# Attention block on one core: query and key projections of two chunks by seven products instead of eight, other order of units, weights read again from DRAM

## Chip, core and metric

The kernel runs on one core of a Trainium2 chip. The metric is device time in microseconds of one execution. Matrix products run on TensorE (PE), elementwise and search work on VectorE (DVE), activations and copies out of PSUM on ScalarE (ACT), more elementwise work on GpSimd (POOL); SyncE (SP) issues nearly all DMAs, in program order.

## The reference

Inputs are `hidden` (4 batches x 1024 rows x 512), weights in float32, and biases. Per batch, cut to what matters here:

```
x = layernorm(hidden)
q  = rope(rmsnorm(x @ Wq  + bq)  * qn_w)      # 512 -> 16 heads x 128
lk = rope(rmsnorm(x @ Wlk + blk) * kn_w)      # 512 -> 16 heads x 128
lv = x @ Wlv + blv
e  = softmax-weighted sums of 4 rows of x     # 256 entries
ck = rope(rmsnorm(e @ Wk + bk)); cv = e @ Wv + bv
sparse: q @ ck / sqrt(128), causal, best 8 entries, softmax, times cv
local:  q @ lk / sqrt(128) over the last 128 positions, softmax, times lv
out = hidden + ((sparse + local) / 2) @ Wo + bo + fp8-rounded x @ fp8-rounded input2
```

## The kernel before

**Chunks and units.** The rows are cut into 32 chunks of 128 (`t`; eight per batch, `c = t % 8`), the 16 heads into eight pairs (`u`). A unit `n = 8 t + u` is one chunk and two heads; there are 256. All weights stay in SBUF: `wqk_sb[u]` holds 512 rows x (256 of Wq, 256 of Wlk), `wlv_sb[u]`, `wo_sb[u]`. The tokens of a chunk, turned, are in `xnT`; `xone` is their first 128 features with one row replaced by ones, for the bias.

**A unit.** `queries` (L606) multiplies the tokens by `wqk_sb[u]`: four matmuls with 512 columns into the PSUM tile `qp`, of which there are two. A float32 matmul appears in the profile as two instructions. `squares` (L321, ScalarE) sums the squares of four heads, `spread` (L315, L316, POOL) turns them into the factors `r`; `normalize` (L634, VectorE) scales `qp` into `th`, `rotate` (L337 on POOL, L339 to L342 on VectorE) applies the angles, `turn_keys` (L687, L690, VectorE) turns blocks of 32x32 into `thb`; SP writes that to DRAM (L695) and reads it back (L705) as `qT` and `lkT`. `scores` (L754, L761, L764) fill `sc`; `weigh` (L786 to L812, VectorE) masks, finds the best eight and their maximum, and ScalarE takes exponentials (L814, L822); `settle` (L830 to L840, VectorE), `divide` (L847, ScalarE); `turn` (L865, VectorE) turns blocks, through DRAM again (L873, L907) into `probT`. `values_of` (L712) makes `vp`, `keep_values` (L724) copies it; `values` (L924) makes the contexts `cp`, `keep_context` (L939) copies them, `to_output` (L957) multiplies by `wo_sb[u]`. PSUM has eight banks: `qp` two, `pp` (values and all short-lived products) two, `sc` two, `ctx` and `out` one each.

**Order.** The order of the instructions on each engine is written out by hand: the loop over steps `s` at the end. Step `s` works on several units at once: scores, weighing, probabilities of unit `s`; normalizing, rotating, turning of `s + 2`; products and squares of `s + 3`; values of `s + 1`; value product of `s - 1`; output of `s - 2`. Every engine goes through its list in order, so a waiting instruction holds what follows it.

**Work once per chunk.** `chunk_prep` (L355 to L432: statistics, normalizing, the weights of the four-row sums) is dealt out over eight steps by the names in `FIRST_HALF` and `SECOND_HALF`; `chunk_eight` with `quantize` (L287 to L298, then L588 and L592) makes the fp8 product, two small parts in each step; `chunk_entries` adds the entries once in four chunks (L536 to L573). In the first eight steps `fold_first_row` (L272) subtracts the first row of each weight matrix and `round_w2` rounds `input2`.

## Time and profile before

| | us |
|---|---|
| median of 3 runs | 2641.59 (2640.97 to 2642.03) |
| span of the profiled execution | 2641.7 |
| VectorE busy in the third batch (643.0 us) | 548.65 |
| ScalarE busy there | 343.79 |
| POOL busy there | 188.74 |
| first eight units after the start, 30 to 123 us | 93.0 |
| second chunk's eight units, 123 to 206 us | 83.0 |

An engine's busy time says how much of a stretch it worked; the waits say which engine it waited for; the timeline gives every instruction's start and length in us. A line such as L606 names the line of the kernel. The times of the profile are of one execution.

### The profile page before, as it was taken

What the parts mean: (1) busy time and instruction counts of PE and PEld (TensorE: products, weight loads), DVE (VectorE), ACT (ScalarE), POOL (GpSimd) and SP (SyncE); (2) the same over time, 40 slices, a digit from 0 to 9 for tenths busy, and PEclk for the clock granted to TensorE, in tenths of its full rate; (3) what the DMA queues carried; (4) which work ended last, traced back from release to release, by engine and by line L of the source; (5) the groups of instructions that cost most, each with busy time, mean ns of one, the idle gap of its engine ahead of it and who ended that gap; (6) DMA issues with size and microseconds to landing.
All of it is one profiled execution on the core that took longest, in us unless ns stands there. A gap on an engine that the chain in (4) does not pass through costs nothing.

```text
span 2641.7 us, 46868 instructions
## 1 busy us (share of the span) xinstructions
PE 2609.3 (99%) x11879; PEld 1784.3 (68%) x11879; DVE 2213.4 (84%) x8381; ACT 1390.9 (53%) x5560; POOL 786.2 (30%) x1128
## 2 busy tenths in 40 slices
PE   8999999999999999999999999999999999999998
PEld 4666666776666666767766666667666666676776
DVE  6888888889888888888888888888888888877886
ACT  3545545555555555555555555555555555555555
POOL 3522323223332223232233322233323322322222
PEclk9999999999999999999999999999999999999999
DMA  8356556666655555666655555666665555566554
GB/s 255 110 156 162 151 145 175 171 176 158 164 143 154 162 155 156 169 173 170 166 157 144 158 149 158 177 164 164 171 176 147 150 148 153 147 168 171 159 152 110
DMA packets 722252, 422.20 MB, mean 160 GB/s; under 512 B 395823, under 2 KB 671552, under 8 KB 721984
## 3 DMA queue, kind: packets, MB, share of 16 engines
q1 hardware_dynamic: 721952, 419.20, 58.8%
q8 instruction: 97, 1.59, 0.3%
q14 instruction: 171, 1.40, 0.2%
q10 hardware_dynamic: 32, 0.02, 0.0%
HBM read 225.80 MB, written 193.20 MB: 159 GB/s over the span
## 4 chain that ended last, share of the span: by engine, by line
PE 84%; DVE 7%; ACT 3%; DMA 3%; SPq 2%; issue 1%; POOL 0%; ACTq 0%; DVEq 0%
PE qp L606 28%; PE op L957 14%; PE vp L712 14%; PE cp L924 13%; PE sc L764 5%; PE sc L761 4%; PE sc L754 4%; ACT prob L847 1%; ACT prob L814 1%; PE fp L588 1%; DVE sc L786 1%; DVE probB L865 1%; PE ep L536 1%; SPq L695 1%; DVE taken L812 1%
## 5 line engine op out<-in xcount | busy, mean ns | idle before, releaser
L606 PE MATMUL qp<-wqk,xnT 128*128 128x512 f32 x1552 | 709.8, 593 | 3.0 <-DMA wqk<-in_L_attn_Wlk_dram 2.4
L814 ACT ACTIVATE prob<-sc,neg 128x256 f32<-128x256 f32 (+1 forms) x512 | 235.9, 461 | 773.3 <-DVE taken L812 744.0
L606 PEld LDWEIGHTS qp<-wqk,xnT 128*128 128x128 f32 x1552 | 295.0, 190 | 372.5 <-issue 368.8
L847 ACT ACTIVATE prob<-prob,tot 128x256 f32<-128x256 f32 (+7 forms) x1024 | 382.0, 443 | 294.5 <-DVE tot L840 294.5
L712 PEld LDWEIGHTS vp<-wlv,xnT 128*128 128x128 f32 x2048 | 389.0, 190 | 161.3 <-issue 116.2
L957 PE MATMUL op<-wo,cT 128*128 128x512 f32 x1024 | 481.6, 593 | 4.2 <-ACT cT L939 4.2
L712 PE MATMUL vp<-wlv,xnT 128*128 128x256 f32 x2048 | 483.6, 379 | 0.0
L337 POOL TENSOR_TENSOR rb<-th,cs 128x256 f32<-128x256 f32 x256 | 203.8, 796 | 740.0 <-DVE th L634 733.2
L786 DVE CUSTOM_DVE_ANT_0 sc<-sc,mask_b 128x256 f32<-128x256 f32 (+1 forms) x512 | 211.6, 414 | 172.7 <-PE sc L764 162.7
L957 PEld LDWEIGHTS op<-wo,cT 128*128 128x128 f32 x1024 | 193.6, 190 | 229.8 <-issue 186.8
L865 DVE STREAM_TRANSPOSE probB<-prob 128x512 f32<-128x512 f32 (+2 forms) x490 | 305.8, 629 | 11.5
L315 POOL TENSOR_SCALAR r<-ss 128x4 f32<-128x4 f32 x256 | 61.9, 242 | 843.3 <-ACT junk L321 840.6
L924 PE MATMUL cp<-probT,lv 128*128 128x128 f32 x1920 | 299.0, 276 | 6.4 <-DMA probT<-pr 4.9
L321 ACT ACTIVATE junk<-qp 128x128 bf16<-128x128 f32 x1024 | 278.6, 272 | 28.9 <-PE qp L614 4.5
L924 PEld LDWEIGHTS cp<-probT,lv 128*128 128x128 f32 x1920 | 272.8, 191 | 25.4 <-issue 9.3
L634 DVE SCALAR_TENSOR_TENSOR th<-qp,r,norm_w 128x128 f32<-128x128 f32 x1024 | 286.1, 342 | 0.7 <-POOL r L316 0.4
L316 POOL TENSOR_TENSOR r<-r,nhalf 128x4 f32<-128x4 f32 x256 | 265.6, 1037 | 21.4
L830 DVE SCALAR_TENSOR_TENSOR prob<-taken,prob 128x128 f32<-128x128 bf16 (+7 forms) x512 | 186.4, 365 | 98.1 <-ACT prob L822 96.6
L606 PE MATMUL qp<-wqk,xone 128*128 128x512 f32 x496 | 258.3, 602 | 0.9 <-DMA xone<-xb_dram 0.7
L924 PE MATMUL cp<-probT,cv 128*128 128x128 f32 x1536 | 255.1, 275 | 0.0
L764 PE MATMUL sc<-ckT,qT 128*128 128x96 f32 (+7 forms) x1024 | 226.4, 303 | 0.0
L924 PEld LDWEIGHTS cp<-probT,cv 128*128 128x128 f32 x1536 | 212.7, 192 | 0.0
(141 smaller groups left out, 3674.9 us busy)
## 6 DMA issues: line engine op xcount, KB each, us to landing
pr<-probB SPq DMA_DIRECT2D x125, 512.0 KB
probT<-pr SPq DMA_DIRECT2D x500, 128.0 KB
qk<-thb SPq DMA_DIRECT2D x992, 64.0 KB
pr<-probB SPq DMA_DIRECT2D x96, 384.0 KB
probT<-pr SPq DMA_DIRECT2D x384, 96.0 KB
qT<-qk SPq DMA_DIRECT2D x248, 128.0 KB
lkT<-qk SPq DMA_DIRECT2D x248, 128.0 KB
x_norm<-_attn_hidden_states_dram SPq DMA_DIRECT2D x32, 256.0 KB
```

The source lines that it names most:

```text
L316: nc.gpsimd.tensor_tensor(r, r, nhalf[: ss.shape[0], 0:n], ALU.pow)
L321: nc.scalar.activation(junk[: src.shape[0]], src, AF.Square, accum_out=acc)
L606: nc.tensor.matmul(qp, xnT[:, k, :] if k or not t else xone, wqk_sb[u][:, k, :], start=(k == 0), stop=(t > 0 and k == KK - 1),)
L634: nc.vector.scalar_tensor_tensor(th[:, i, :], qp[:, ts(i, D)], r[:, i : i + 1], norm_w[:, i // 2, :], ALU.mult, ALU.mult,)
L712: nc.tensor.matmul(vp[:, 0:256], xnT[:, k, :], wlv_sb[u][:, k, :], start=(k == 0), stop=(k == KK - 1),)
L764: nc.tensor.matmul(sc[:, spa], q, ckT[:, 0:m], start=True, stop=True)
L786: nc.vector.tensor_tensor_reduce(sc[h][:, loc], sc[h][:, loc], mask_b[:, loc], -1.0, TAKEN, ALU.add, ALU.min, neg[h][0],)
L814: nc.scalar.activation(probs[h][:, loc], sc[h][:, loc], AF.Exp, bias=neg[h][0], scale=-1.0, accum_out=tot[:, h, 0:1],)
L847: nc.scalar.mul(probs[h][:, cols], probs[h][:, cols], tot[:, h, part : part + 1])
L865: nc.vector.transpose(pb[:, :, ds(h * g, g), :], prob[:, parts[0] * P : (parts[-1] + 1) * P].rearrange("p (g b i) -> p b g i", b=NB, i=BLK),)
L924: nc.tensor.matmul(blocks(cp[:, h, :]), v, probT[:, :, h * len(parts) + i - parts[0], :], start=(i == parts[0]), stop=(i == parts[-1]),)
L957: nc.tensor.matmul(op, cT[:, h, :], wo_sb[u][:, h, :], start=(u == 0 and h == 0), stop=(u == NU - 1 and h == 1),)
```

## The change

The first 16 units (chunks 0 and 1) are done as before. From unit 16 on, units go in pairs: `place(n)` alternates between chunk `2p` and chunk `2p + 1` with the same heads. For the 120 pairs, the tokens of two chunks (256 rows) times `wqk_sb[u]` are seen as 2x2 blocks, 128 rows x 256 features times 256 features x 256 columns, and made of seven block products by Strassen's algorithm in Winograd's form, each two matmuls of 256 columns. `first_products` makes four of them in an even step `s` (for units `s + 4` and `s + 5`), into the two banks `qk_banks`; `first_sums` copies them to the `th` tiles of both units and adds on POOL. `second_products` makes three in the odd step, into the same banks; `second_sums` adds them on VectorE. `squares` and `normalize` then read `th` in SBUF instead of `qp` in PSUM.

The four sums of token blocks are made by `sum_tokens` once for two chunks on POOL. The four sums of weight blocks are made once by `combine_weights` in steps 4 to 8 on POOL, written to DRAM and read back for each pair by `load_combined` (four transfers of 256 KB); the freed parts of `wqk_sb` (`places`) hold them. `wo_sb` has two tiles instead of eight, and `load_wo` reads 512 KB for each pair.

PSUM: `qk_banks` two, `out_banks` two (two chunks' outputs grow side by side), `sc` two, `vc_bank` holds `vp` and `cp` in its halves, `pp` has one bank, and until step 11 also the second output bank. `th`, `lkT`, `lv` and `x` come from hand-made pools, `th` from one of three tiles that gives out the tile last returned. Preparation of chunks starts at the steps in `prep_at`, later the steps `16 p - 2` and `16 p + 5`. Matmuls of the last, partly filled block of entries use only its filled rows.

```diff
-        return work.tile(list(shape), dtype, tag="scratch", name=name, bufs=2)
+        return work.tile(list(shape), dtype, tag="scratch", name=name, bufs=4)
+
+    def bank(name):
+        return psum.tile([P, 512], F32, tag=name, name=name, bufs=1)
+
+    qk_banks = [bank("qk_0"), bank("qk_1")]
+    out_banks = [bank("out_0"), bank("out_1")]
+    vc_bank, pp_bank = bank("vc"), bank("pp")
+    spare_banks = [pp_bank, out_banks[1]]
 
     def pp(name):
-        return psum.tile([P, 512], F32, tag="pp", name=name, bufs=2)
+        spare_banks.append(spare_banks.pop(0))
+        return spare_banks[-1]
...
+    class Pool:
+
+        def __init__(self, tiles, last=0):
+            self.free, self.taken, self.last = list(tiles), {}, last
+
+        def take(self, key):
+            self.taken[key] = self.free.pop(self.last)
+            return self.taken[key]
+
+        def give(self, key):
+            self.free.append(self.taken.pop(key))
...
-    wqk_sb = [const.tile([P, KK, 512], F32, name=f"wqk_{u}") for u in range(NU)]
+    wqk_sb = [const.tile([P, 2, 2, 2, 256], F32, name=f"wqk_{u}") for u in range(NU)]
...
-    wo_sb = [const.tile([P, 2, HID], F32, name=f"wo_{u}") for u in range(NU)]
+    wo_sb = [const.tile([P, 2, HID], F32, name=f"wo_{i}") for i in range(2)]
+    wo_of = {}
+
+    def row_of_weights(u, k):
+        return wqk_sb[u][:, k // 2, :, k % 2, :]
 
...
-    def load_wo(u, engine):
-        engine.dma_start(wo_sb[u], Wo[ts(u, 256), :].rearrange("(h p) n -> p h n", p=P))
+    def load_wo(n, engine):
+        _, u = place(n)
+        w = wo_sb[n % 2 if n < FIRST else n // 2 % 2]
+        wo_of[n] = w
+        if n >= FIRST:
+            wo_of[n + 1] = w
+        engine.dma_start(w, Wo[ts(u, 256), :].rearrange("(h p) n -> p h n", p=P))
...
+    combined = [
+        dram.tile([4, P, 512], F32, tag=f"combined_{u}", name=f"combined_{u}", bufs=1)
+        for u in range(NU)
+    ]
+
+    def flat(v):
+        return v.rearrange("p k n -> p (k n)")
+
+    def combine_weights(u):
+        (b11, b12), (b21, b22) = (
+            [flat(wqk_sb[u][:, j, i]) for i in range(2)] for j in range(2)
+        )
+        one, two = (v.rearrange("p h d -> p (h d)") for v in th_tiles[1:])
+        sub = nc.gpsimd.tensor_tensor
+        sub(one, b12, b11, ALU.subtract)
+        nc.sync.dma_start(combined[u][0], one)
+        sub(two, b22, one, ALU.subtract)
+        nc.sync.dma_start(combined[u][1], two)
+        sub(one, b21, two, ALU.subtract)
+        nc.sync.dma_start(combined[u][3], one)
+        sub(two, b22, b12, ALU.subtract)
+        nc.sync.dma_start(combined[u][2], two)
+
+    places = [flat(wqk_sb[u][:, 0, 1]) for u in range(NU)]
+    token_sums = [
+        v.rearrange("p (k s) -> p k s", k=2)
+        for at in places[4:6]
+        for v in (at[:, 0:256], at[:, 256:512])
+    ]
+
+    def load_combined(u, which):
+        for i in which:
+            nc.sync.dma_start(places[i], combined[u][i])
+
+    def sum_tokens(p, which):
+        (a11, a12), (a21, a22) = ((b[:, 0:3:2, :], b[:, 3:5, :]) for b in (x_bufs(2 * p), x_bufs(2 * p + 1)))
+        s1, s2, s3, s4 = token_sums
+        op = nc.gpsimd.tensor_tensor
+        if which == 0:
+            op(s3, a11, a21, ALU.subtract)
+            op(s1, a21, a22, ALU.add)
+            op(s2, s1, a11, ALU.subtract)
+        else:
+            op(s4, a12, s2, ALU.subtract)
...
+    th_tiles = [const.tile([P, 4, D], F32, name=f"th_{i}") for i in range(3)]
+    sums = const.tile([P, 256], F32, name="sums")
...
-        return divmod(n, NU)
+        if n < FIRST:
+            return divmod(n, NU)
+        p, r = divmod(n, FIRST)
+        return 2 * p + r % 2, r // 2
...
+        "th": Pool(th_tiles[::-1], -1),
...
     def queries(n):
         t, u = place(n)
         xnT, xone = chunks[t]
-        qp = psum.tile([P, 512], F32, tag="qp", name=f"qp_{n}")
+        qp = qk_banks[n % 2] if n != FIRST - 1 else out_banks[1]
...
+    def product(to, a, b):
+        for k in range(2):
+            nc.tensor.matmul(to, a[k], b[:, k, :], start=k == 0, stop=k == 1)
...
+    def first_products(p, u):
+
+        xa, one = chunks[2 * p]
+        s1, s2, s3, _ = token_sums
+        t1, t2, t3, _ = (v.rearrange("p (k n) -> p k n", k=2) for v in places[:4])
+        lo, hi = qk_banks
+        product(lo[:, 0:256], (one, xa[:, 1, :]), wqk_sb[u][:, 0, 0])
+        product(hi[:, 256:512], both(s1), t1)
+        product(lo[:, 256:512], both(s2), t2)
+        product(hi[:, 0:256], both(s3), t3)
+
+    def second_products(p, u):
+        xa, xb = chunks[2 * p][0], chunks[2 * p + 1][0]
+        lo, hi = qk_banks
+        product(lo[:, 0:256], both(xa[:, 2:4, :]), wqk_sb[u][:, 1, 0])
+        product(hi[:, 0:256], both(xb[:, 2:4, :]), places[3].rearrange("p (k n) -> p k n", k=2))
+        product(hi[:, 256:512], both(token_sums[3]), wqk_sb[u][:, 1, 1])
+
+    def quarters(n):
+        return [
+            units[i]["th"].rearrange("p h d -> p (h d)")[:, ts(j, 256)]
+            for i in (n, n + 1)
+            for j in range(2)
+        ]
+
+    def first_sums(n):
+
+        for i in (n, n + 1):
+            units[i] = {"th": pools["th"].take(i)}
+        c11, c12, c21, c22 = quarters(n)
+        lo, hi = qk_banks
+        nc.scalar.copy(c11, lo[:, 0:256])
+        nc.scalar.copy(c22, lo[:, 256:512])
+        nc.scalar.copy(c21, hi[:, 0:256])
+        nc.scalar.copy(c12, hi[:, 256:512])
+        nc.gpsimd.tensor_tensor(sums, c11, c22, ALU.add)
+        nc.gpsimd.tensor_tensor(c21, c21, sums, ALU.add)
+        nc.gpsimd.tensor_tensor(c22, c21, c12, ALU.add)
+        nc.gpsimd.tensor_tensor(c12, c12, sums, ALU.add)
+
+    def second_sums(n):
+        c11, c12, c21, _ = quarters(n)
+        lo, hi = qk_banks
+        nc.vector.tensor_tensor(c11, c11, lo[:, 0:256], ALU.add)
+        nc.vector.tensor_tensor(c21, c21, hi[:, 0:256], ALU.add)
+        nc.vector.tensor_tensor(c12, c12, hi[:, 256:512], ALU.add)
...
     def squares(n, heads):
         w = units[n]
+        w["ss"] = work.tile([P, 4], F32, tag="ss", name=f"ss_{n}")
+        src = w["qp"] if "qp" in w else w["th"]
         for i in heads:
-            square_sum(w["ss"][:, i : i + 1], w["qp"][:, ts(i, D)], f"{n}_{i}")
+            square_sum(w["ss"][:, i : i + 1], src[:, i, :], f"{n}_{i}")
 
     def spread(n):
         w = units[n]
...
 
     def normalize(n):
         w = units[n]
-        qp, r = w.pop("qp"), w["r"]
-        th = work.tile([P, 4, D], F32, tag="th", name=f"th_{n}", bufs=1)
+        r = w["r"]
+        if "qp" in w:
+            qp, th = w.pop("qp"), pools["th"].take(n)
+        else:
+            qp = th = w["th"]
         for i in range(4):
             nc.vector.scalar_tensor_tensor(
                 th[:, i, :],
-                qp[:, ts(i, D)],
+                qp[:, i, :],
                 r[:, i : i + 1],
...
+        pools["th"].give(n)
...
-        vp = pp(f"vp_{n}")
+        vp = vc_bank[:, 0:256]
...
-        cp = psum.tile([P, 2, P], F32, tag="ctx", name=f"cp_{n}", bufs=1)
+        cp = vc_bank[:, 256:512].rearrange("p (h q) -> p h q", h=2)
...
+                    v, rows = cv[i - 2], min(P, m - P * (i - 2))
                 nc.tensor.matmul(
                     blocks(cp[:, h, :]),
-                    v,
-                    probT[:, :, h * len(parts) + i - parts[0], :],
+                    v[0:rows],
+                    probT[0:rows, :, h * len(parts) + i - parts[0], :],
...
+    prep_at = {1: -1, 2: 6, 3: 8, 4: 13, 5: 16, 6: 19, 7: 22}
+    prep_at.update(
+        {2 * p + 4 + i: FIRST * p - 2 + 7 * i for p in range(2, NT // 2 - 2) for i in range(2)}
+    )
...
+    x_sum_at, eight_at, tokens_at, angles_at = {3: 0, 11: 1}, {5: 0, 13: 1}, {2: 1}, {}
+    for p in range(1, NT // 2):
+        x_sum_at.update({FIRST * p + 3: 2 * p, FIRST * p + 10: 2 * p + 1})
+        eight_at.update({FIRST * p + 3: 2 * p, FIRST * p + 11: 2 * p + 1})
+        tokens_at.update({FIRST * p - 8: 2 * p, FIRST * p - 7: 2 * p + 1})
+        angles_at.update({FIRST * p - 8: 2 * p, FIRST * p - 7: 2 * p + 1})
+    eight_at.pop(FIRST * (NT // 2 - 1) + 11)
 
...
+        pair, odd = divmod(s + 4, 2)
+
+        strassen = pair >= NU and pair < NN // 2
+        pair_of = divmod(pair, NU)
...
+        if s >= FIRST - 5:
+            if r == FIRST - 5 and p + 1 < NT // 2:
+                sum_tokens(p + 1, 0)
+            if r == FIRST - 4 and p + 1 < NT // 2:
+                sum_tokens(p + 1, 1)
...
-        if u == 7 and t in made:
+        if s + 3 < FIRST:
+            for_unit(s + 3, (queries,))
+        if strassen and s != FIRST - 4:
+            (second_products if odd else first_products)(*pair_of)
...
             turn(s)
         if s + 2 >= NU:
             for_unit(s + 2, (turn_keys,))
+        if strassen:
+            (second_sums if odd else first_sums)(2 * pair)
         steps()
-        host = t if u < 4 else t + 1
-        if host in ready and s >= -2:
...
         for_unit(s + 3, (squares, (0, 1, 2, 3)), (spread,))
         for_unit(s - 2, (to_output,))
...
+        if 0 <= s <= FIRST:
+            load_wo(s, nc.sync)
+        elif s > FIRST and odd:
+            load_wo(s + 1, nc.sync)
...
+        for v in {4: (0, 1), 5: (2, 3), 6: (4, 5), 7: (6,), 8: (7,)}.get(s, ()):
+            combine_weights(v)
+        if s == FIRST - 5:
+            load_combined(0, range(4))
+            spare_banks[:] = [pp_bank]
+        if strassen:
+            if odd:
+                load_combined((pair_of[1] + 1) % NU, (3,))
+            else:
+                load_combined((pair_of[1] + 1) % NU, (0, 1, 2))
```

## The prediction

> **What bounds the kernel now.** I read the page's busy lines first, then the table of stretches for the third batch (chunks 0 to 7 of 128 rows, eight units each), then the waits, then the timeline of single units.
>
> ```profile
> span 2641.7 us, 46868 instructions
> PE 2609.3 (99%) x11879; PEld 1784.3 (68%) x11879; DVE 2213.4 (84%) x8381; ACT 1390.9 (53%) x5560; POOL 786.2 (30%) x1128
> q1 hardware_dynamic: 721952, 419.20, 58.8%
> L606 PE MATMUL qp<-wqk,xnT 128*128 128x512 f32 x1552 | 709.8, 593 | 3.0 <-DMA wqk<-in_L_attn_Wlk_dram 2.4
> L712 PE MATMUL vp<-wlv,xnT 128*128 128x256 f32 x2048 | 483.6, 379 | 0.0
> L606 PE MATMUL qp<-wqk,xone 128*128 128x512 f32 x496 | 258.3, 602 | 0.9 <-DMA xone<-xb_dram 0.7
> ```
>
> TensorE never rests. A matmul of these shapes shows as two instructions, and their ends overlap, so the price is busy time over count: 512 columns (709.8 + 258.3) / 2048 = 0.473 us, 256 columns 483.6 / 2048 = 0.236 us. The price goes with the columns.
>
> ```profile
> 1356.30:1426.60 70.30, 69.79 (x300) 45.80 (x299) 59.59 (x261) 36.97 (x172) 22.67 (x35) 1.00 0.55 148
> 1426.60:1504.10 77.50, 77.50 (x353) 52.42 (x353) 63.81 (x260) 41.64 (x172) 22.43 (x33) 1.00 0.55 153
> ...
> 1827.20:1911.50 84.30, 84.30 (x391) 58.76 (x390) 74.30 (x261) 44.95 (x172) 24.36 (x33) 1.00 0.64 168
> 1911.50:1999.30 87.80, 87.66 (x398) 60.68 (x397) 76.67 (x267) 46.71 (x176) 25.80 (x37) 1.00 0.62 165
> ```
>
> Columns: stretch, length, then busy time of PE, weight loads, VectorE (DVE), ScalarE (ACT), GpSimd (POOL), clock, DMA share, GB/s. These are chunks 0, 1, 6 and 7; 2 to 5 take 78.1, 80.4, 81.3 and 83.3. Two units, one of each chunk of a pair, so take 18.48, 19.81, 20.58 and 21.51 us for the pairs (0,1), (2,3), (4,5), (6,7); the mean is 643 / 32 = 20.09.
>
> ```profile
> DVE sc L786 <- PE sc L764: 162.7, 166, 2.1
> DVE prob L830 <- ACT prob L822: 96.6, 248, 1.2
> ```
>
> These are VectorE's main waits: for TensorE's scores only 162.7 us in all, 0.6 a unit, and 0.39 us a unit for the exponentials. VectorE, in order, is nearly a second bound.
>
> ```profile
> 1399.94 0.30 DVE L786 CUSTOM_DVE_ANT_0 sc<-sc,mask_b 128x128 f32<-128x128 f32 x1 [1.99 <-PE sc L764]
> 1401.92 1.12 DVE L634 SCALAR_TENSOR_TENSOR th<-qp,r,norm_w 128x128 f32<-128x128 f32 x4
> 1403.12 0.73 POOL L337 TENSOR_TENSOR rb<-th,cs 128x256 f32<-128x256 f32 x1 [3.49 <-DVE th L634]
> 1405.44 0.25 ACT L321 ACTIVATE junk<-qp 128x128 bf16<-128x128 f32 x1
> 1406.27 0.40 DVE L690 STREAM_TRANSPOSE thb<-th 128x256 f32<-128x256 f32 x1
> 1407.07 0.20 POOL L315 TENSOR_SCALAR r<-ss 128x4 f32<-128x4 f32 x1 [3.22 <-ACT junk L321]
> 1407.35 1.05 POOL L316 TENSOR_TENSOR r<-r,nhalf 128x4 f32<-128x4 f32 x1
> ```
>
> One unit of chunk 0 on the timeline (start, length). VectorE weighs scores (L786 to L634, 1.98 us), normalizes and rotates unit n+2 and turns it (L634 to the end of L690, 4.75 us). ScalarE squares and POOL's root r for unit n+3 end at 1408.40, 2.2 us before the next L634 at 1410.64: no cost now.
>
> **The change, part by part.** *TensorE.* A pair's queries and keys go from 16 instructions of 512 columns to 28 of 256: 16 x 0.473 - 28 x 0.236 = 0.96 us less. 120 of the 128 pairs use it: 115 us off an otherwise full TensorE.
>
> *What takes its place.* Per pair, ScalarE gets four 128x256 copies out of PSUM (0.28 us apart, as keep_keys' two copies start in the timeline), POOL four 128x256 sums (0.73 each, the L337 shown), VectorE three sums with one operand in PSUM (0.40 for the first, as L547 with 397 ns, 0.33 for each next, as L687 to L690). Normalizing from SBUF saves 0.11 us a unit (L558, the same operation from SBUF, 314 ns against 342, four times). By busy time all fits: VectorE 2213 + 120 x (1.06 - 0.22) = 2314 us.
>
> The order decides. Call a step even when it issues first_products. Four facts of the changed order: (1) first_products needs the banks that second_sums of the step before has read, and second_sums stands behind VectorE's turn_keys. (2) The buffer into which the first copy goes is the one that turn_keys of the same step has just read, since the pool of three hands out the last one returned; so ScalarE's four copies, and behind them its squares of unit s+3, values and contexts, wait for the end of turn_keys. (3) POOL's four sums wait for two copies and stand ahead of r of unit s+3. (4) VectorE's normalize of s+3, in the odd step, waits for that r, and all its later work is queued behind it; TensorE and the SP queue's stores wait for that in turn. So a pair is one chain:
>
> a. First VectorE sum to normalize, even step: 0.09 (to ScalarE) + 1.54 (four squares, 1405.44 to 1406.98) + 0.10 (squares from SBUF, 306 ns against 272) + 0.09 + 1.33 (r, 1407.07 to 1408.40) + 0.04 = 3.2 us; or the two other sums 0.66 and the weighing, if longer. The weighing, from the fourth unit of each chunk: 1.98, 2.38, 2.52, 2.65, 2.78, 2.91, 3.04, 3.17. So 3.2, 3.2, 3.44, 3.70 for the four pairs.
> b. Normalize to end of turn_keys, even chunk: 4.75, 5.26, 5.82, 5.91, less 0.11.
> c. End of turn_keys to the odd normalize: 0.09 + 0.65 (two copies) + 0.09 + 4 x 0.73 + 3 x 0.08 (the gap of L315 to L316) + 0.08 + 1.33 + 0.04 = 5.45.
> d. The odd chunk's normalize to turn_keys: 5.18, 5.34, 5.76, 6.07, less 0.11 and 0.39, since the exponentials are now ready in time.
> e. First of second_sums: 0.45 with its hand-over.
>
> Sums: 18.42, 19.09, 20.31, 20.97, mean 19.70.
>
> Work that comes once per chunk is on top. VectorE's chunk work in even steps hides in c (5.45 against 2.4 to 3.2 of weighing); in odd steps it stands between second_sums and the weighing. By the groups that is, per 16 units: 2.74 (chunk started in an even step: normalize and turn 1.24, exponentials 0.85, sum 0.65), 2.83 (the other: statistics 0.85, logits 0.73, weights 1.25), two quantizations 2.62, a last sum 0.68: 8.87, or 1.11 a pair, less 0.14 of slack in pair (0,1): 0.97. The second POOL operation of a quantization (1.27) stands between the sums and r, twice per 16 units: 0.32 a pair, of which I take half, since VectorE has chunk work of its own there. A pair: 19.70 + 0.97 + 0.16 = 20.83 against 20.09, 0.74 more; 120 pairs: 89 us.
>
> *POOL against VectorE.* Beside POOL's work L634, one operand in PSUM, ranges from 335 to 352 ns; L830, both in SBUF, from 178 to 1358. Normalize now has both in SBUF. Six POOL operations of quantizations per 16 units start as r ends. Bounds: 0, as L634 now, to 6 x 1.18 / 8 = 0.89 a pair, 106 us. I take 0, as most of r's ends have nothing behind them; the upper end goes into the range.
>
> [...]
>
> [...]
>
> *Start.* combine_weights: 32 POOL operations of 128x512 (1.27, L294) are 41 us in steps 4 to 8, each a unit of 10.4 (the second chunk's 83.0 / 8) in which POOL has 3.1 already. Steps 4 to 6: 10.2 + 3.1 - 10.4 = 2.9 over, three times, 9 us; if each reused buffer waits for its store (2.5 us, twice a weight), 27 or more. Bounds 0 to 35; I take 10.
>
> *At nothing:* weights from DRAM (1 MB of sums and 0.5 MB of Wo a pair, five SP issues of some 0.45 us in a pair whose SP now issues 10 us of 20), asked for two steps ahead; covered by that distance, priced below. The changed places of preparation, one spare bank, and values sharing a bank with contexts are covered by c; uncovered, a wait of TensorE costs its own length in even steps. Fewer rows in the last value matmuls save nothing: columns set the price.
>
> Total: 2641.7 + 89 + 10 = **2740**, made against the profiled 2641.7, which is 0.1 from the median 2641.59.
>
> **Rivals.** *TensorE stays the bound:* 2641.7 - 115 + 10 = 2537, faster. For it: 99% busy and the busy sums. Against: c. It needs a pair's chain at TensorE's 19.13 even with chunk work, 1.7 us shorter. [...]
> *Chunk work hides in the chain's waits:* 19.70 a pair, 120 x 0.39 = 47 less: 2605. Against: facts 1 and 4 leave none in odd steps.
> *DMA becomes the bound:* 189 MB in 92,000 packets more; by packets the 58.8% becomes 66, by bytes 85. If the probabilities then land 1 us past need in each unit, 240 us: 2880. For: the share. Against: they land about 2 us ahead (stored 2 us before the end of an even step, 6.5 to land, used about 6.6 into the odd one).
> *The products are not fewer:* the changed order shows seven products of two matmuls, so this is out.
>
> **How the numbers follow.** Chain with chunk work 0.66 (2680 to 2830), chunk work hidden 0.12, TensorE 0.10, DMA 0.07, break-even 0.05. The range 2600 to 2830 leaves out TensorE's case and DMA's. A difference under 0.2% (5 us) can't be told from none: faster 0.22, same 0.05, slower 0.73.
>
> **What would show it.** Right: POOL's r and VectorE's normalize alternate between early and late; in odd steps VectorE idles 1 to 2 us before normalize, released by POOL's r; ScalarE's first copy waits for turn_keys; TensorE's first product waits for VectorE; TensorE's share falls to 92 to 94%. Wrong: TensorE still 98% or more busy, or POOL's sums done before turn_keys ends, or probT landings as the main wait.

## The result, and the profile after

The changed kernel takes 3063.97 us (median of 4 runs, 3061.54 to 3068.1) against 2641.28 us before in the same job: a ratio of 1.1603, 95% interval 1.1587 to 1.162. The forecast was 2740 us: right in the direction, wrong by a factor of four in the size (+99 against +423), and outside its range. The profiled execution has a span of 3059.8 us. From its page (engine: busy us, share, instructions; queue: packets, MB, share; the chain by engine):

```profile
span 3059.8 us, 52706 instructions
PE 2744.9 (90%) x13266; PEld 2145.8 (70%) x13301; DVE 2385.6 (78%) x8741; ACT 1566.6 (51%) x6032; POOL 1203.3 (39%) x1686
q1 hardware_dynamic: 828176, 621.15, 70.8%
DVE 33%; PE 22%; ACT 13%; DMA 10%; POOL 10%; issue 6%; SPq 5%; ACTq 0%; POOLq 0%; DVEq 0%
```

No engine is full any more: TensorE went from 99% to 90%, and the chain that ends last runs through all of them. TensorE's busy time has even grown, from 2609.3 to 2744.9 us, though 115 us were to be saved: its mean granted clock is 0.957 of full speed against 0.999, and partly filled matmuls turned out dearer (below). The waits that the forecast had named, from the view of waits (us in total, times, longest):

```profile
POOL sums L782 <- ACT th L779: 427.9, 107, 10.9
...
DVE th L432 <- POOL rb L428: 164.2, 22, 9.7
PE qk L742 <- DVE th L790: 149.5, 79, 5.5
DVE sc L969 <- PE sc L945: 125.8, 73, 14.9
...
ACT th L778 <- DVE thb L867: 120.0, 109, 1.4
DVE th L813 <- POOL r L407: 98.5, 89, 3.7
...
POOL wqk L356 <- DMA tokens<-xb_dram: 67.7, 8, 10.4
...
PE vc L1114 <- DMA probT<-pr: 17.4, 21, 2.0
```

ScalarE's first copy waits for the turned keys in 109 of 120 pairs, TensorE's first product for the second sums, VectorE's normalization for `r`: three links of the forecast chain. New are VectorE's wait for `rb`, 7.5 us a time, and POOL's for `tokens`: the longest of the waits for `rb` come where a sum of tokens stands ahead of it on POOL (e1).

One of the shorter pairs, chunks 4 and 5, fifth place of eight (the two steps in which the fifth pair of heads is weighed), as rows of the timeline of VectorE, ScalarE and POOL (start, us, instruction, idle before it and its releaser):

```profile
2047.60 0.38 DVE L790 TENSOR_TENSOR th<-th,qk 128x256 f32<-128x256 f32 x1
...
2048.56 0.67 DVE L494 SCALAR_TENSOR_TENSOR products<-x,wcmp_sb 128x512 f32<-128x512 f32 x1
...
2049.17 0.43 DVE L969 CUSTOM_DVE_ANT_0 sc<-sc,mask_b 128x256 f32<-128x256 f32 x1
...
2051.94 1.13 DVE L813 SCALAR_TENSOR_TENSOR th<-th,r,norm_w 128x128 f32<-128x128 f32 x4
...
2057.15 0.40 DVE L870 STREAM_TRANSPOSE thb<-th 128x256 f32<-128x256 f32 x1
...
2057.34 0.37 ACT L778 COPY th<-qk 128x256 f32<-128x256 f32 x1 [1.18 <-DVE thb L867]
...
2058.06 0.73 POOL L782 TENSOR_TENSOR sums<-th,th 128x256 f32<-128x256 f32 x1 [4.15 <-DVE row L499]
...
2061.56 1.01 POOL L407 TENSOR_TENSOR r<-r,nhalf 128x4 f32<-128x4 f32 x1
...
2062.61 1.14 DVE L813 SCALAR_TENSOR_TENSOR th<-th,r,norm_w 128x128 f32<-128x128 f32 x4 [0.22 <-POOL r L407]
...
2063.83 0.77 POOL L428 TENSOR_TENSOR rb<-th,cs 128x256 f32<-128x256 f32 x1 [1.25 <-DVE th L813]
...
2064.16 0.66 DVE L1013 SCALAR_TENSOR_TENSOR prob<-taken,prob 128x192 f32<-128x192 bf16 x1
...
2068.25 0.38 DVE L790 TENSOR_TENSOR th<-th,qk 128x256 f32<-128x256 f32 x1
```

Read from one L790 to the next this is the forecast's chain: 0.38 for the first sum, 3.96 to the even normalization (a), 5.61 to the end of the turned keys (b), 5.06 through copies, sums and `r` to the odd normalization (c), 5.72 to the end of the next turned keys (d), less 0.08 by which the next L790 begins before that end: 20.65 us in all. This pair has chunk work too: the logits of a chunk (L494) stand ahead of the weighing, which takes 2.77 us from L969 on, and a is 3.96 where the forecast without chunk work has 3.44. So where did the time come from? Taking the same distance for all pairs by their place among the eight of a chunk pair gives the table that settles most (us, means of 14 or 15 pairs each, without the first pair and the last sixth one, which has no sum of tokens; the last column is the mean of all pairs):

| place | 1 | 2 | 3 | 4 | 5 | 6 | 7 | 8 | mean |
|---|---|---|---|---|---|---|---|---|---|
| changed kernel | 20.94 | 21.58 | 24.19 | 24.29 | 20.36 | 28.67 | 23.65 | 21.98 | 23.19 |
| e1, tokens early | 21.01 | 21.82 | 24.20 | 24.30 | 20.42 | 23.44 | 24.09 | 22.00 | 22.68 |
| e14, fourth buffer | 20.40 | 21.41 | 23.28 | 23.36 | 20.20 | 28.93 | 22.65 | 21.06 | 22.64 |
| e15, no first sums | 20.27 | 21.23 | 22.76 | 21.79 | 20.01 | 30.07 | 22.98 | 20.63 | 22.42 |
| e17, chunk work ahead | 20.93 | 21.95 | 23.70 | 21.62 | 21.30 | 28.76 | 23.31 | 21.73 | 22.88 |

The forecast mean was 20.83, of which 1.13 for work that comes once per chunk. No place is free of chunk work: every one has some on VectorE, and the fifth has at least the logits. The best place, 20.36, is 0.66 above the forecast's 19.70 without chunk work; the excess of the other places over it is 22.8 us in eight pairs, 2.85 a pair. The first sixteen units, from the first weighing to that of unit 16, take 249 us against 176 before.

### The profile page after: what moved, and what is told of

It is laid out like the page before. It is cut to its first block, busy times and chain, and to the rows that moved or that the text cites. A ratio compares the mean times of both kernels' runs of the same rounds, so it can differ in the third digit from the quotient of the medians.

```text
span 3059.8 us, 52706 instructions
## 1 busy us (share of the span) xinstructions
PE 2744.9 (90%) x13266; PEld 2145.8 (70%) x13301; DVE 2385.6 (78%) x8741; ACT 1566.6 (51%) x6032; POOL 1203.3 (39%) x1686
## 3 DMA queue, kind: packets, MB, share of 16 engines
q1 hardware_dynamic: 828176, 621.15, 70.8%
## 4 chain that ended last, share of the span: by engine, by line
DVE 33%; PE 22%; ACT 13%; DMA 10%; POOL 10%; issue 6%; SPq 5%; ACTq 0%; POOLq 0%; DVEq 0%
PE qk L742 7%; ACT prob L1030 6%; DVE probB L1048 4%; PE vc L1114 4%; DMA pr<-probB 3%; PE out L1145 3%; PE vc L893 3%; DVE prob L1013 3%; DVE sc L969 3%; ACT prob L997 3%; DVE th L813 3%; DVE taken L995 2%; SPq L1097 2%; DVE top L990 2%; POOL r L407 2%
## 5 line engine op out<-in xcount | busy, mean ns | idle before, releaser
L742 PE MATMUL qk<-wqk,tokens 128*128 128x256 f32 x1440 | 396.5, 411 | 203.9 <-DVE th L790 149.5
L1145 PE MATMUL out<-wo,cT 128*128 128x512 f32 x1024 | 498.5, 610 | 43.7 <-ACT cT L1130 39.7
L893 PEld LDWEIGHTS vc<-wlv,tokens 128*128 128x128 f32 x2048 | 394.8, 193 | 172.0 <-issue 125.3
L893 PE MATMUL vc<-wlv,tokens 128*128 128x256 f32 x2048 | 490.8, 383 | 4.7 <-ACT lv L905 4.7
L742 PE MATMUL qk<-wqk,wqk 128*128 128x256 f32 x1860 | 483.2, 408 | 5.0 <-DMA wqk<-combined 5.0
L412 ACT ACTIVATE junk<-th 128x128 bf16<-128x128 f32 x960 | 299.4, 312 | 307.9 <-DVE th L790 284.9
L742 PEld LDWEIGHTS qk<-wqk,wqk 128*128 128x128 f32 x1860 | 388.2, 209 | 70.2 <-issue 5.9
L813 DVE SCALAR_TENSOR_TENSOR th<-th,r,norm_w 128x128 f32<-128x128 f32 x960 | 306.7, 380 | 98.5 <-POOL r L407 98.3
L1114 PE MATMUL vc<-probT,lv 128*128 128x128 f32 x1920 | 314.2, 283 | 18.9 <-DMA probT<-pr 17.4
L969 DVE CUSTOM_DVE_ANT_0 sc<-sc,mask_b 128x256 f32<-128x256 f32 (+1 forms) x510 | 209.5, 411 | 134.8 <-PE sc L945 125.8
L1114 PE MATMUL vc<-probT,cv 128*128 128x128 f32 (+3 forms) x1536 | 293.2, 291 | 0.0
L1013 DVE SCALAR_TENSOR_TENSOR prob<-taken,prob 128x96 f32<-128x96 bf16 (+7 forms) x512 | 209.5, 423 | 52.5 <-ACT prob L1005 49.0
```

Of the source, the lines that this page charges most:

```text
L412: nc.scalar.activation(junk[: src.shape[0]], src, AF.Square, accum_out=acc)
L742: nc.tensor.matmul(to, a[k], b[:, k, :], start=k == 0, stop=k == 1)
L813: nc.vector.scalar_tensor_tensor(th[:, i, :], qp[:, i, :], r[:, i : i + 1], norm_w[:, i // 2, :], ALU.mult, ALU.mult,)
L893: nc.tensor.matmul(vp, xnT[:, k, :], wlv_sb[u][:, k, :], start=(k == 0), stop=(k == KK - 1),)
L969: nc.vector.tensor_tensor_reduce(sc[h][:, loc], sc[h][:, loc], mask_b[:, loc], -1.0, TAKEN, ALU.add, ALU.min, neg[h][0],)
L1013: nc.vector.scalar_tensor_tensor(probs[h][:, spa], taken[:, h, 0:m], TAKEN_FROM, probs[h][:, spa], ALU.is_ge, ALU.mult, accum_out=tot[:, h ...
```

## The experiments

Unless another base is named, each starts from the changed kernel (3064 us); the kernel before was run beside each and took 2641 to 2643 us.

**e1: tokens a step earlier.** Through line L356 POOL waits for tokens whose fetch SP issued only at the end of the step before.

```diff
-        tokens_at.update({FIRST * p - 8: 2 * p, FIRST * p - 7: 2 * p + 1})
+        ahead = 8 if p == 1 else 9
+        tokens_at.update({FIRST * p - ahead: 2 * p, FIRST * p - ahead + 1: 2 * p + 1})
```

> Edit: from the third pair of chunks on, the turned tokens of a pair of chunks are fetched one step earlier (steps 16p-9 and 16p-8 instead of 16p-8 and 16p-7); nothing else. In the changed kernel's trace POOL's first sum of tokens waits some 7.6 us for this transfer in step 16p+11, and VectorE's rotation, whose factor stands behind it on POOL, waits with it. Theory A (the queue of POOL carries the wait to everything): that stall goes in 14 of 15 places, about 8 us each, so 100 to 115 us less: 2950 to 2965. Theory B (repeated transfers from DRAM are what slows the kernel, and the stall is only where it shows): the transfer is late all the same or the time comes back elsewhere: above 3030. Theory C (units in pairs and the shared banks are the cost): within 20 us of 3064.

Measured: 3004.08 us (2998.95 to 3007.52), 60 less, between theories A and B. The sixth pair falls from 28.67 to 23.44 us. In the changed kernel that pair looks like this (timeline of SP, POOL and VectorE):

```profile
2088.28 1.60 SPq L595 DMA_DIRECT2D tokens<-xb_dram  x4
...
2091.52 0.73 POOL L356 TENSOR_TENSOR wqk<-tokens,tokens 128x256 f32<-128x256 f32 x1 [7.62 <-DMA tokens<-xb_dram]
...
2093.69 0.72 POOL L428 TENSOR_TENSOR rb<-th,cs 128x256 f32<-128x256 f32 x1
2094.45 0.29 DVE L432 TENSOR_TENSOR th<-thb,rb 128x128 f32<-128x128 f32 x1 [7.94 <-POOL rb L428]
```

The sum of tokens isn't urgent, but it stands ahead of `rb` on POOL, and VectorE's rotation waits for `rb`. 5.2 us in each of 14 sixth pairs is 73; the other places give some 12 back.

**e2: the weight sums of the start spread**, one weight a step.

```diff
-        for v in {4: (0, 1), 5: (2, 3), 6: (4, 5), 7: (6,), 8: (7,)}.get(s, ()):
-            combine_weights(v)
+        if 4 <= s < 12:
+            combine_weights(s - 4)
```

> Edit: the sums of weight blocks are made for one weight tile per step, steps 4 to 11, instead of two, two, two, one, one in steps 4 to 8. The first 16 units take 249 us in the changed kernel against 176 before. If POOL's work and its waits for the stores of the two buffers hold the start (theory A), spreading them saves 25 to 50 us: 3015 to 3040. If the start is slow for its transfers or its banks, less than 10 us.

Measured: 3066.55 us, no gain. The first eight units get shorter (12.91 us each against 15.49), the next eight longer (18.02 against 15.69): in six of the eight steps POOL now waits 4.5 to 11.3 us for a store, whose issue stands at the end of SP's list. So the wait seems to come once per step, and there are more steps.

**e3: no repeated loads.** Weight sums and output weights are not loaded again after the first pairs (that part is left out, so the products are of other weights).

```diff
-        engine.dma_start(w, Wo[ts(u, 256), :]...)
+        if n < FIRST + 4:
+            engine.dma_start(w, Wo[ts(u, 256), :]...)
...
-        if strassen:
-            ... load_combined(...)
```

> Edit: the sums of weights are read from DRAM once and the output weights are not read any more after unit 19; 1.5 MB per pair of units of reading are left out. The output is then not the reference's, since all pairs but the first use wrong weights; the work of all engines is the same. Theory B (transfers): 150 us or more less, at most 2915. Theory A: 0 to 40 us less, 3025 to 3064, mostly from the tokens landing sooner in step 16p+11; the pairs without that stall keep their 21 to 24 us.

Measured: 3025.65 us, ratio 1.1449 (1.1432 to 1.1466): the loads cost 38 us, not the bulk.

**e4: units in pairs, but queries and keys without Strassen** (`strassen = False`, `queries` in every step, no weight or token sums).

> Edit: everything of the change but Strassen's products: units in pairs of chunks, shared banks, output weights read per pair, preparation at its new steps; queries and keys by four matmuls of 512 columns for every unit as before, no sums of weights or tokens. Theory C (pairs and banks are the cost): 2900 or more. Theory A (the chain through the sums is the cost): TensorE is the bound again, 2635 to 2690.

Measured: 2742.55 us, ratio 1.0379 (1.0364 to 1.0395), TensorE 99% busy: outside both ranges, nearer to theory A's. Without Strassen's products and what feeds them 321 of the 423 us are gone; 101 are left in a kernel that TensorE bounds. The groups by shape of the changed kernel show one cause of these (busy us, mean ns, idle time before):

```profile
L1114 PE MATMUL vc<-probT,cv 128*128 128x128 f32 x768 | 138.5, 276 | 0.0
L1114 PE MATMUL vc<-probT,cv 32*128 32x128 f32 x256 | 62.5, 324 | 0.0
L1114 PE MATMUL vc<-probT,cv 64*128 64x128 f32 x256 | 62.1, 322 | 0.0
...
L1114 PEld LDWEIGHTS vc<-probT,cv 32*128 32x128 f32 x256 | 37.8, 184 | 15.7 <-issue 0.5
```

A matmul of 32 or 64 rows is not the same as one of 128: it shows 322 to 324 ns against 276, and its weight load has idle time in front of it (15.7 us in 256) where the full one has none. A group of eight value matmuls, four of them of 32 rows, takes 1.56 us in the timeline, from its start to the start of what follows, where eight full ones take 0.89 (e5, and the kernel before); with 64 rows it is the same 0.67 more, 86 us in the 128 units of chunks with 32 or 64 such rows. 96 rows cost as 128: 274 ns, and 1.34 us for a group of twelve either way.

**e5: full rows.** The columns that the other chunk of the pair leaves behind are zeroed on POOL, and the whole tiles once a batch.

```diff
-                    v, rows = cv[i - 2], min(P, m - P * (i - 2))
+                    v, rows = cv[i - 2], min(P, m - P * (i - 2)) if n >= NN - 2 else P
...
+        if s >= FIRST and odd:
+            m = columns(s)[1]
+            for prob in probs:
+                nc.gpsimd.memset(prob[:, 2 * P + m - NE : 2 * P + m], 0.0)
```

> The changed kernel, but the matmuls of the last, partly filled block of entries use all 128 rows again; the 32 columns of weights that the other chunk of the pair leaves behind are set to zero on POOL in every odd step (two small memsets, after the spread). Theory A (a matmul of 32 or 64 rows keeps its weight load from overlapping: in the trace 0.67 us a unit in chunks 0, 1, 4 and 5, 128 units, 86 us of TensorE): all the groups of value matmuls of 8, 12 and 16 instructions go to 0.89, 1.34 and 1.78 us, and the time falls by something between 43 (only the even steps' share lies on the chain) and 86 us: 2978 to 3021 us. Theory B (the chain over DVE, ACT and POOL alone sets the end, and TensorE has slack): below 20 us.

Measured: 3069.98 us, no gain. TensorE's busy time falls by 57 us (2744.9 to 2687.5), POOL's grows by 19 with the zeroing (1203.3 to 1222.7), and the two weren't separated; that TensorE has slack in the changed kernel (90% busy) fits.

**e7: e4 and full rows together.**

> Units in pairs of chunks, no Strassen, and full rows in the last block: two of the changed kernel's parts are taken out together. If partly filled rows explain what the pairs without Strassen lost against the kernel before (2742.55 against 2642), this is 2742.55 - 86 = 2657 us, 2645 to 2670; if the order of units in pairs itself costs something, 2700 us or more.

Measured: 2670.63 us (2665.02 to 2672.55), 72 less than e4: where TensorE is full, the same edit counts nearly whole. What is left to the kernel before, 28 us, is the other order of units, the shared banks and the Wo loads; it wasn't split further.

**e6: second sums right behind the normalization** of the odd step.

```diff
         for_unit(s + 2, (normalize,))
+        if strassen and odd:
+            second_sums(2 * pair)
```

> The changed kernel, but VectorE does the three second sums of the odd step right behind the normalization of the same step, not behind the turned keys. Theory A (one chain through DVE, ACT, POOL and DVE sets the pair): the stretch from the second sums to the even normalization (mean 4.30 us of 23.13) leaves the chain, until TensorE (busy 21 us of a pair, some of it at a lowered clock) sets the pair: 21 to 21.8 us a pair, 2800 to 2900 us. Theory B (TensorE's own even step, 11.3 us from the first of the four products to the end of the scores, holds the normalization back nearly as long): the stretch is filled by a wait of TensorE and the gain is under 60 us.

Measured: 3030.21 us, 34 less: inside theory B. VectorE's wait for scores grows from 125.8 to 185.3 us.

**e8: four mends together**, those of e1, e5 and e6, and in even steps squares and spread ahead of the first sums.

> Strassen with four mends at once: tokens fetched a step earlier, squares and spread of the even step ahead of the first sums, second sums right behind the normalization, full rows. If the chain and the partly filled rows are all that holds the changed kernel, TensorE becomes its bound: its busy 21 us of a pair less 0.67 in most pairs less what the lowered clock adds, about 20 us, with the first sixteen units' 249 us unmended: 2640 to 2700 us. [...]

Measured: 2966.43 us (2961.43 to 2972.21), far above the 2640 to 2700 expected. VectorE's wait for `r` is gone (98.5 to 2.2 us in the groups), and yet a pair takes 22.4 us. The chain has moved:

```profile
PE 27%; DVE 26%; DMA 21%; SPq 9%; ACT 7%; issue 6%; POOL 4%; ACTq 0%; DVEq 0%; POOLq 0%
```

DMA and SP's issues, 15% of the changed kernel's chain, are 30% of this one.

**e9, e11, e12: the loads in the gap**, ahead of the fetch of the turned weights, where SP waits for a store: e9 on the changed kernel, e11 on e8, e12 on e11 with the weight sums of the start one a step, two of the four stores ahead of the fetch.

```diff
+        if s > FIRST and odd:
+            load_wo(s + 1, nc.sync)
+        if strassen:
+            ... load_combined(...)
         if by_dma(s):
             fetch(s)
```

> The changed kernel, but the SP queue issues the loads of weight sums and of output weights ahead of the fetch of the turned weights, while that fetch waits for its store to land, and not behind it. Theory S (the SP queue's list of issues and landings, about 11 us a step, is nearly the step itself, and the added loads lie at its end): on the changed kernel alone, where the queue still waits 700 us for VectorE's stores, a gain of 10 to 40 us: 3025 to 3055. Theory T (the queue has slack, only the DVE-ACT-POOL chain counts): within 10 us of 3064.

> The four mends and the loads in the gap. Theory S: most of what leaving the loads out gives, 2800 to 2900. Theory T: 2955 to 2975.

> The four mends, the loads in the gap, and the weight sums of the start one weight a step, with the first two stores issued ahead of the fetch and the other two sums at the step's end. If POOL's waits for the stores were what made the first sixteen units 249 us instead of 176, the run is 40 to 70 us below the run with the loads in the gap alone; if the start is held by the sums themselves or by the stores' place in the queue anyhow, below 15 us.

Measured: 3246.94, 3173.56 and 3179.78 us, e9 183 slower than the changed kernel, e11 207 slower than e8: a miss of both theories. In e9's groups (idle before them, last column):

```profile
L1114 PE MATMUL vc<-probT,lv 128*128 128x128 f32 x1920 | 356.1, 310 | 287.4 <-DMA probT<-pr 262.4
```

SP was free to issue, but the 0.75 MB stood in the same queue ahead of the fetch, and TensorE waits 262.4 us for the turned weights (17.4 in the changed kernel). e12's first sixteen units take 235 us against 248 in e11, which is lost again later.

**e10: e8 without the repeated loads** (left out as in e3).

> The four mends of the run before (2966) and no repeated loads of weight sums and output weights (left out of the computation: the products take whatever sums lie in the place, so the result is another). Theory S (after the mends the chain goes through the SP queue and the landings: 9% and 21% of it): 5 issues a pair and their waits go, 100 to 200 us: 2770 to 2870. Theory T (DMA is worth what it was worth to the changed kernel, 38 us): about 2930.

Measured: 2847.62 us: 119 less, against 38 on the changed kernel. The same transfers are three times as dear once the chain in front of them is shorter.

**e16: the loads from ScalarE's queue**, on e8.

```diff
-            nc.sync.dma_start(places[i], combined[u][i])
+            nc.scalar.dma_start(places[i], combined[u][i])
...
-            load_wo(s + 1, nc.sync)
+            load_wo(s + 1, nc.scalar)
```

> The four mends (2966), with the repeated loads of weight sums and output weights issued by ScalarE into a queue of its own. Leaving them out gave 119 us there, putting them ahead of the fetch cost 207. If the order in one queue is what they cost (a fetch stands behind 0.75 to 1 MB), most of it comes back: 2860 to 2910. If it is the bytes, which the 16 engines must move in any queue, nothing: 2950 to 2980; ScalarE's five issues a pair can cost 20 to 60 more.

Measured: 3085.8 us, 119 slower than e8 and beyond both ranges. TensorE waits 292.7 us for the turned weights (102.6 in e8). A second queue does not make the bytes cheaper here: the two take 72.0% of the 16 engines together, 52.5 and 19.5, of a span of 3088.7 us, where SP's queue takes 73.5% of 2967.2 in e8. Why the turned weights then come later was not shown; how much of the 119 is the lost order of the one queue and how much ScalarE's own time for issuing wasn't separated.

**e13: the start without weight sums** (the weights themselves are stored in their place, so the sums are left out).

> The changed kernel without POOL's 32 weight sums of the start: the weights themselves are stored in the place of their sums, 32 stores as before (the sums are left out, so the result is another). If POOL's sums and the waits of POOL for their stores make the first sixteen units 249 us instead of 176, this gives 55 to 75 us: 2990 to 3010. If the stores on the SP queue or the pairs' own beginning make it, under 25 us.

Measured: 3030.54 us, 34 less, between the two ranges, and 212 us for the first sixteen units: POOL's sums and their waits make 37 of the 73. The other half stays in the second eight (14.77 us each, 10.38 before) with a wait for scores; its cause is open.

**e14: a fourth `th` buffer**, given out in turn; `sums` moves into the buffer of `rb` (at the start it runs over the scratch of the weight sums, so these are partly overwritten).

```diff
-    th_tiles = [const.tile([P, 4, D], F32, name=f"th_{i}") for i in range(3)]
+    th_tiles = [const.tile([P, 4, D], F32, name=f"th_{i}") for i in range(4)]
...
-        "th": Pool(th_tiles[::-1], -1),
+        "th": Pool(th_tiles[::-1], 0),
```

> The changed kernel with a fourth th buffer, given out in turn, so that ScalarE's copies of the first products no longer wait for turn_keys. The chain of the prediction takes that wait as its link (waits of ScalarE for thb: 120 us, 109 times, 1.1 each). If the link sets the pair: 60 to 120 us less, 2945 to 3005, and the stretch from the turned keys to the odd normalization shrinks by 0.5 to 1.1. If ScalarE's order of work or TensorE holds the copies as long: under 20 us.

**e15: no first sums**: the four POOL operations of `first_sums` are left out.

> The changed kernel without POOL's four sums of 256 columns behind the copies (they are left out, so the result is another). The chain: r of the odd step comes up to 4 x 0.73 = 2.9 us sooner, so with nothing else in the way 2.9 x 120 = 350 us less, to TensorE's and VectorE's own bound near 2700. If TensorE's even step holds the scores nearly as long (it needs 11.3 us from the first product to the scores), 60 to 150 us less, and VectorE waits for the scores in place of r.

Measured: e14 3017.73 us (46 less, between its two ranges, with a start that is 19 us longer), e15 2969.41 us (95 less, within its second range). The stretch c, 6.13 us in the mean, falls to 5.42 and 4.94. Both links help to set the pair, so the chain was real; but 2.9 us of POOL taken out shorten c by 1.2 and the pair by 0.75, since the scores are hardly earlier: VectorE's wait for them grows from 125.8 to 154.4 and 140.6 us, and sixth pairs lengthen by up to 1.4.

**e17: chunk work ahead** of the copies and sums in even steps.

```diff
-        if strassen:
-            (second_sums if odd else first_sums)(2 * pair)
+        if strassen and odd:
+            second_sums(2 * pair)
         steps()
         prepare(s, 0)
+        if strassen and not odd:
+            first_sums(2 * pair)
```

> The changed kernel, but in even steps the chunk work (the steps of quantization and entries, the preparation) is issued ahead of the four copies and sums, not behind them. Pairs without chunk work take 20.4 us, near the forecast; the third, fourth and seventh pair of a chunk pair take 24.2, 24.3 and 23.7. If the chunk work costs there because its POOL operations stand between the four sums and r (a quantization add, 1.27 us) or behind the sums with ScalarE and VectorE waiting for them (the means), the fourth pair falls by about 3 us and the third and seventh by about 1.2: 15 x 5.4 = 81 us, with what TensorE gives back 50 to 80 less: 2985 to 3015. [...]

Measured: 3024.68 us, 39 less, short of the 50 to 80 expected. The fourth pair falls by 2.67 us, near the 3 expected; the third and seventh by 0.49 and 0.34, not 1.2, and the fifth, where the chunk's row now stands ahead of the copies, grows by 0.94. What the fourth pair waited for, in the changed kernel (timeline):

```profile
2035.73 0.72 POOL L785 TENSOR_TENSOR th<-th,sums 128x256 f32<-128x256 f32 x1
2036.42 0.23 POOL L454 TENSOR_SCALAR off<-lnst 128x1 f32<-128x1 f32 x1
2036.68 0.72 ACT L455 ACTIVATE x<-x,off 128x512 f32<-128x512 f32 x1 [2.88 <-POOL off L454]
...
2037.58 0.21 POOL L458 TENSOR_SCALAR off<-off 128x1 f32<-128x1 f32 x1 [0.93 <-ACT x L455]
...
2037.82 0.55 DVE L463 TENSOR_SCALAR x<-x,off,lnr 128x512 f32<-128x512 f32 x1 [4.38 <-POOL off L458]
```

A mean of one column stands behind the four sums; ScalarE, with the squares of the next unit queued behind L455, waits 2.88 us for it, and VectorE, with the weighing queued behind L463, 4.38. In the third pair c fell too, 6.56 to 5.12, but the displaced POOL operations now meet VectorE in b (5.46 to 6.41).

**e18: six mends** (e8, e14's buffer from step 11 on, e17).

> A version meant to be fast: tokens a step earlier, second sums right behind the normalization, chunk work and squares of the even step ahead of the copies and sums, full rows, a fourth th buffer given out in turn from step 11 on. Against the four mends (2966): if the chunk work's place and the buffer still hold there, 2880 to 2930; if the queue of transfers holds (leaving the repeated loads out gave 119 us there), 2940 to 2980. Under 2641, the kernel before, it can't come by any of the readings: VectorE's own work is 19 us a pair.

Measured: 2907.62 us (2899.28 to 2912.67), ratio 1.1002 (1.0978 to 1.1026). The best version with all of the computation, and still 10% slower than the kernel before.

## Why the prediction was wrong

*"The order decides", the links a to c: right.* Waits and e14 and e15 show the chain, and the fifth and first places, where almost none of the chunk work is on POOL, take 20.4 and 20.9 us. c was given 5.45 and is 5.2 and 5.4 there. Signs named in the forecast came: the first copy waits for the turned keys, TensorE for the second sums, and VectorE idles 1.1 us for `r` in 89 pairs; TensorE's share fell further than to 92%.

*d, "less 0.11 and 0.39": wrong, 0.50 a pair, 60 us.* The medians of d are 5.22, 5.37, 5.76 and 6.05 for the four pairs of chunks, the trace of before with nothing taken off. Normalizing from SBUF saves nothing. From the view of line L813 (ns: minimum, median, maximum):

```profile
L813 DVE SCALAR_TENSOR_TENSOR th<-th,r,norm_w x960: 334/344/1358, 256.2 to 3024.9; 128x128 f32<-128x128 f32 x192
...
L813 DVE SCALAR_TENSOR_TENSOR th<-qk,r,norm_w x60: 340/343/351, 19.6 to 223.1; 128x128 f32<-128x128 f32 x60
```

The median is the same from SBUF and from PSUM; the 314 ns row that I had used was another operation's mean. The wait for the exponentials did shrink in odd units, from 0.37 to 0.14 us (means over the records of units 32 to 249), but POOL's `rb` now runs beside the work behind it: the second L1013 of an odd unit takes 0.58 us in the mean (0.42 before) and L1022 0.41 (0.36 before). The two rows at 2063.83 and 2064.16 above show it: 0.66 us beside `rb`, 0.35 for the L1013 ahead of it.

*"Work that comes once per chunk": the term that failed, 1.13 a pair forecast, some 3.3 measured, about 260 us.* The places lie 2.85 a pair above the best one, and the best one's a, 3.88 us in the mean against a forecast of 3.39, has up to 0.5 of chunk work in it (L494). "VectorE's chunk work in even steps hides in c" looked at VectorE's busy time alone. The work is a sequence over POOL, ScalarE and VectorE, and many of its POOL operations now stand in a queue with something long: behind the four sums (fourth pair, 3.9 us above the best place, 2.7 of it taken off by e17), ahead of `rb` with a transfer to wait for (sixth pair, 8.3 us, 5.2 of it taken off by e1), and, by the timeline alone, between sums and `r` and then beside VectorE (third and seventh, 7.1 us together). e1 and e17, each by itself, give 60 and 39 us back; for the rest, above all the quantization's share, the cause is argued from places and waits, and no run took it out.

*"POOL against VectorE", taken at 0:* too low. VectorE's busy time was forecast as 2314 us and is 2385.6; of these 72 more, 26 are the gain of normalizing from SBUF that never came. In the changed kernel L813 reaches 1358 ns (352 at most before), 70 of its 1024 above 400, and each of these 70 runs beside a POOL operation; 67 of the 1024 before did so too, with one operand in PSUM, and none was long. In e18, where the mean with both inputs in SBUF is 431 ns (380 in the changed kernel), 199 are above 400. In the rows of L813 above only the form with both inputs in SBUF is ever long, 1358 ns at most against 351; no run shows what holds it beside POOL's work. So what the upper end stood for is there, at a third of its size: L813's mean over all 1024 rose from 342 to 378 ns, 36 us of busy time against 106.

*"Start, I take 10": 73*, beyond its own upper bound of 35. e13 shows 37 of them to be POOL's sums and their waits, about what that bound stood for; the other 36 lie in the second eight units, for which the forecast had no term, and their cause is open.

*"At nothing: weights from DRAM": 38 us on the changed kernel, 119 on e8* (e3, e10). "Fewer rows ... save nothing" was costed at nothing in the wrong direction: it costs 72 us where TensorE is full (e7), and nothing that e5 could show here.

*TensorE's 115 us.* They never came. Its matmuls for queries and keys take 408 to 411 ns in the mean in the changed kernel, 388 to 393 in e8 and 379 at best (L712's 256 columns before). Around the 3.5 us wait at 2093.6 the windows show the granted clock (columns: window, length, busy of PE, PEld, DVE, ACT and POOL, clock, DMA share, GB/s):

```profile
2091.00:2096.00 5.00, 2.64 (x19) 2.17 (x18) 1.55 (x4) 0.00 (x0) 2.82 (x4) 1.00 0.46 156
2096.00:2101.00 5.00, 3.83 (x12) 3.14 (x13) 4.79 (x18) 2.39 (x11) 1.98 (x3) 0.74 0.65 207
2101.00:2106.00 5.00, 5.00 (x20) 3.57 (x19) 4.54 (x19) 2.98 (x10) 1.90 (x3) 0.92 1.08 292
2106.00:2111.00 5.00, 5.00 (x34) 4.41 (x33) 2.29 (x7) 3.64 (x16) 2.70 (x4) 1.00 0.60 196
```

After the pause TensorE is busy and slow: 0.74, then 0.92, then 1.00 again; in windows of 1 us it is 0.69, 0.50, 0.50 and 0.60 from 2098 to 2102. Kernels that hardly pause (e4, before, both 99% busy) have 0.999. That stall and clock go together here is what the rows show; no run held the clock while it kept the stalls.

*The account.* Up to the first weighing of unit 16 the changed kernel takes 279.4 us against 206.3, 73 more where 10 were forecast. From there to the end it takes 2780.4 against 2435.4, 345 more where 89 were forecast. The two misses, 63 and 256, are the 319 of the span. By the table the pairs alone missed by (23.19 - 20.83) x 120 = 283 us; 18 of the 27 over 256 come from the base, since the kernel before takes 20.24 us a pair over all these units and not the 20.09 of its third batch. Of the 283 about 260 are chunk work. The chain without it was nearly right, some 19.9 against 19.70, in part by luck: d was 0.50 too short and c 0.29 too long. *Rivals:* TensorE stays the bound, chunk work hidden and DMA bound are out: TensorE is at 90%, the chunk work is the largest miss, and without the loads 3026 us remain. e8 and e10 show the DMA rival as what comes next.

## What to carry to other kernels

When an edit turns a full engine into a chain over several in-order queues, price every small operation by what stands ahead of it in its queue and what stands behind the engine that waits for it; work that "fits" by busy time can cost most there. The gains of mends to a balanced pipeline do not add, and a cost depends on what stands in front of it: full rows in the value matmuls were worth 0 in one kernel and 72 us in another, the same loads 38 and 119. Before moving bulk loads into an idle slot of a queue, ask which urgent transfer then stands behind their bytes.

## What the runs showed of the hardware

In a stream of float32 matmuls of 128 rows, one of 32 or 64 rows cost more than a full one: 0.67 us for four in a group, with idle time ahead of the weight load (15.7 us in 256 of 32 rows, 15.4 in 256 of 64), and 96 rows cost as 128 (1.34 us for a group of twelve either way). VectorE's normalization of 128x128 with both inputs in SBUF (L813), 344 ns in the median, took up to 1358 ns beside POOL's work; with one operand in PSUM it never took more than 352. Loads moved ahead of the fetch of the turned weights cost 183 and 207 us (e9, e11), and moved to a second issuing queue 119 us (e16), with the queues' share at 75.3% in e9 and 72.0% in e16 (70.8% in the changed kernel, 73.5% in e8).
